# One-hot attention by row maxima and a gather in place of the dense softmax product, with the dense path behind a branch

## The chip, the core and the metric

The kernel runs on one core of a Trainium2 chip, in one launch. The metric is the device time of a launch in microseconds (us). Engines: TensorE (PE, with its weight loads PEld), VectorE (DVE), ScalarE (ACT), GpSimd (POOL) and SyncE (SP); the core's 16 DMA engines move data between HBM and the on-chip memory.

## The reference

```python
def _L0_gnn_ref(h, adj_mat, W, a):            # N = 4096, 4 heads, 512 features
    ht = (h @ W).reshape(N, N_HEADS, N_HIDDEN).transpose(1, 0, 2)
    src = jnp.einsum('hnd,hd->hn', ht, a_src)
    dst = jnp.einsum('hnd,hd->hn', ht, a_dst)
    e = jax.nn.leaky_relu(src[:, :, None] + dst[:, None, :], SLOPE) + adj_mat[None]
    att = jax.nn.softmax(e, axis=-1)
    h_prime = jnp.einsum('hij,hjd->hid', att, ht)
    return h_prime.mean(axis=0)
x = _layernorm(x + _L0_gnn_ref(x, adj, L0_gnn_W, L0_gnn_a), axis=-1)
```

`x` is 4096x512, `adj` 4096x4096, `W` 512x2048, all float32. `adj` enters the scores as an added number. It is zero but for about 17 entries of a row in the mean (the diagonal among them), and those are drawn evenly from 0.05 to 1e9. The scores differ by a few units beside that, so in each row the softmax weight of the column with the largest entry rounds to one and all others to zero, as long as the largest entry leads the second by more than the scores can differ. Over the inputs that the reference makes (seed 0), the smallest lead of any of the 4096 rows is 10,880.

## The kernel before, in words

The kernel computes the dense attention. `x` (32 blocks of 128 rows, 8 MB) stays on chip. The first part (lines 62 to 118) makes the two score vectors: `v = W_h a_h` on VectorE (L83), transposes of `x` (L94), products with `v` (L101), and copies of `dst` to all partitions (L107, L108).

The second part works in units: a block of 128 rows of one head, 32 x 4 = 128 units. A unit's scores are made in 8 chunks of 512 columns: `src + dst` on ScalarE (L153), leaky ReLU (L154) and the sum with `adj` and its row maximum on VectorE (L156), the exponential on ScalarE (L168). TensorE then turns each chunk (`transpose`, L173), the turned chunk is copied out of PSUM (L176 on ScalarE, L178 on VectorE), and `apply` (L186) multiplies it with `x`: 32 products of 128x128 by 128x512 a unit. `scale` divides by the sum (L197), `turn` transposes the result (L202), `project` multiplies by the head's columns of `W` (L211) and, after the fourth head, adds `x` and takes mean and variance (L217 to L224); `store` normalises (L230, L231) and writes the block from GpSimd's queue (L232).

The order is written by hand: in the loop at line 244 a unit's transposes and products stand between the last steps of the unit before it and the score making of the next. `load_adj` (L134) fetches four tiles of 128x1024 of `adj` for a block of rows on SP's queue; each is fetched as soon as VectorE has read the tile before it for the fourth head.

## Time and profile before

| | |
|---|---|
| median of 3 runs | 4705.16 us (4705.05 to 4705.61) |
| span of the profiled execution, first to last instruction | 4702.5 us |
| what the median has beside that span | 2.7 us |
| TensorE busy | 4596.1 us, 98% |
| VectorE, ScalarE, GpSimd busy | 2124.3, 1811.9, 18.2 us |
| moved by DMA over the span | 92.66 MB, mean 20 GB/s |
| granted TensorE clock, mean | 0.992 |

The page gives no time of the profiled execution beside its span; sums are made against the span, and the 2.7 us that the median lies above it are added at the end. Busy shares are of the whole span; a stretch's own figures come from the table by stretch. A busy TensorE in this profile is modelled, since its matmuls overlap; the distance of one matmul's start to the next tells more.

### The profile page before, as it was taken

The numbers are of one execution on the slowest core, as the hardware profiler recorded it, in microseconds if no ns is written. First come the engines' busy times: TensorE is split into PE (matmuls) and PEld (weight loads), VectorE is DVE, ScalarE is ACT, GpSimd is POOL, SyncE is SP. The second block draws the span as 40 slices with busy tenths as digits, with TensorE's granted clock in tenths as the row PEclk, the third lists the DMA queues.
The fourth block names the chain that finished last, engine by engine and source line by source line (L and its number), as shares of the span: only waits on it lengthen the run. The fifth ranks groups of instructions, "written<-read, shape, count | busy, mean of one in ns | idle before, by whom it ended". The sixth has DMA issues, their size and how long they took to land.

```text
span 4702.5 us, 38848 instructions
## 1 busy us (share of the span) xinstructions
PE 4596.1 (98%) x14112; PEld 2251.0 (48%) x14112; DVE 2124.3 (45%) x4656; ACT 1811.9 (39%) x3712; POOL 18.2 (0%) x38
## 2 busy tenths in 40 slices
PE   7899999999999999999999999999999999999999
PEld 3344444444444444444444444444444444444444
DVE  3444444444444444444444444444444444444443
ACT  1334334334334434433433433433433443343342
POOL 0000000000000000000000000000000000000000
PEclk7999999999999999999999999999999999999999
DMA  3000000000000000000000000000000000000000
GB/s 125 27 12 21 18 21 20 12 12 21 18 21 20 7 16 21 18 21 16 7 21 21 18 21 16 7 21 21 18 21 12 12 21 21 18 21 12 12 21 3
DMA packets 26127, 92.66 MB, mean 20 GB/s; under 512 B 2768, under 2 KB 2768, under 8 KB 25296
## 3 DMA queue, kind: packets, MB, share of 16 engines
q1 hardware_dynamic: 22656, 75.51, 4.7%
q0 software_dynamic: 2560, 8.39, 0.5%
q10 hardware_dynamic: 720, 6.29, 0.3%
q8 instruction: 111, 1.82, 0.2%
q14 instruction: 80, 0.66, 0.0%
HBM read 81.79 MB, written 8.39 MB: 19 GB/s over the span
## 4 chain that ended last, share of the span: by engine, by line
issue 75%; PE 23%; DVE 1%; POOL 0%; DMA 0%; ACT 0%; POOLq 0%; ACTq 0%; DVEq 0%
PE y_ps L186 16%; PE o_ps L211 2%; PE pt_ps L173 2%; PE ps_b L107 1%; PE ps_sd L101 1%; PE ps_x L94 0%; DVE y L197 0%; DVE prod L83 0%; PE yt_ps L202 0%; POOL out_dram L232 0%; DMA w_sb<-in_L_gnn_W_dram 0%; DVE s L154 0%; DVE sd L103 0%; DVE s L156 0%; PE ps_s L111 0%
## 5 line engine op out<-in xcount | busy, mean ns | idle before, releaser
L186 PE MATMUL y_ps<-x_sb,pt 128*128 128x512 f32 x8192 | 3685.7, 593 | 0.0
L186 PEld LDWEIGHTS y_ps<-x_sb,pt 128*128 128x128 f32 x8192 | 1487.1, 190 | 1531.3 <-issue 1530.9
L154 DVE SCALAR_TENSOR_TENSOR s<-s 128x512 f32<-128x512 f32 x1024 | 705.6, 689 | 1048.4 <-ACT s L153 1006.2
L153 ACT ACTIVATE s<-dst_b,src 128x512 f32<-128x512 f32 x1024 | 723.0, 718 | 971.2 <-PE pt_ps L173 952.2
L178 DVE COPY pt<-pt_ps 128x512 f32<-128x512 f32 x640 | 442.6, 692 | 997.4 <-PE pt_ps L173 997.4
L168 ACT ACTIVATE s<-s,nm 128x512 f32<-128x512 f32 x1024 | 724.0, 708 | 181.0 <-DVE nm L164 181.0
L173 PEld LDWEIGHTS pt_ps<-ident,s 128*128 128x128 f32 x4096 | 512.5, 141 | 551.7 <-issue 538.7
L176 ACT COPY pt<-pt_ps 128x512 f32<-128x512 f32 x384 | 225.1, 586 | 1346.4 <-PE pt_ps L173 1346.4
L156 DVE CUSTOM_DVE_ANT_0 s<-s,adj 128x512 f32<-128x512 f32 x1024 | 708.6, 692 | 35.1
L173 PE MATMUL pt_ps<-ident,s 128*128 128x128 f32 x4096 | 615.3, 273 | 12.7 <-ACT s L168 12.7
L211 PE MATMUL o_ps<-w_sb,yt 128*128 128x512 f32 x1024 | 460.8, 593 | 0.7 <-ACT yt L204 0.7
L211 PEld LDWEIGHTS o_ps<-w_sb,yt 128*128 128x128 f32 x1024 | 184.6, 190 | 184.6 <-issue 183.6
L197 DVE TENSOR_SCALAR y<-y_ps,rz 128x512 f32<-128x512 f32 x128 | 96.0, 750 | 296.8 <-PE y_ps L186 296.8
L168 ACT ACTIVATION_READ_ACCUMULATOR s<-s,nm 128x1 f32 x1024 | 191.2, 187 | 0.0
L202 PE MATMUL yt_ps<-ident,y 128*128 128x128 f32 x512 | 83.9, 286 | 52.6 <-DVE y L197 52.6
L204 ACT COPY yt<-yt_ps 128x512 f32<-128x512 f32 x128 | 75.0, 586 | 76.0 <-PE yt_ps L202 76.0
L202 PEld LDWEIGHTS yt_ps<-ident,y 128*128 128x128 f32 x512 | 53.6, 140 | 83.5 <-DVE y L197 83.5
L224 ACT ACTIVATE sd<-sd 128x1 f32<-128x1 f32 x32 | 6.5, 203 | 210.8 <-DVE sd L223 210.8
L156 DVE DVE_READ_ACCUMULATOR2_ANT m<- 128x1 f32 x1024 | 83.8, 82 | 0.0
L217 DVE TENSOR_TENSOR y<-o_ps,x_sb 128x512 f32<-128x512 f32 x32 | 22.1, 692 | 90.2 <-PE o_ps L211 90.2
L94 PE MATMUL ps_x<-ident,x_sb 128*128 128x128 f32 x128 | 29.9, 422 | 21.8 <-DMA x_sb<-in_x_dram 16.6
L95 ACT COPY xT<-ps_x 128x512 f32<-128x512 f32 x32 | 18.7, 586 | 76.8 <-PE ps_x L94 76.8
(31 smaller groups left out, 412.8 us busy)
## 6 DMA issues: line engine op xcount, KB each, us to landing
adj<-in_adj_dram SPq DMA_DIRECT2D x128, 512.0 KB, 3.4
x_sb<-in_x_dram SPq DMA_DIRECT2D x8, 1024.0 KB, 17.9
out_dram<-y POOLq DMA_DIRECT2D x32, 256.0 KB, 2.3
w_sb<-in_L_gnn_W_dram ACTq DMA_DIRECT2D x4, 1024.0 KB, 10.7
a_b<-in_L_gnn_a_dram ACTq DMA_DIRECT2D x1, 2048.0 KB, 8.8
```

Source lines behind the costliest of these rows:

```text
L153: nc.scalar.activation(s, dst_b[:, h, ts(c, C)], AF.Identity, bias=src[:, ib, h : h + 1])
L154: nc.vector.scalar_tensor_tensor(s, s, SLOPE, s, op0=OP.mult, op1=OP.max)
L156: nc.vector.tensor_tensor_reduce(out=s, in0=s, in1=adj_t[ib, k][:, ts(part, C)], scale=1.0, scalar=LOWEST, op0=OP.add, op1=OP.max, accum_o ...
L168: nc.scalar.activation(s, s, AF.Exp, bias=self.nm, accum_out=self.z[:, c : c + 1])
L173: nc.tensor.transpose(ps[:, q, :], self.s[c][:, ts(q, P)], ident)
L176: nc.scalar.copy(pt, ps)
L178: nc.vector.tensor_copy(pt, ps)
L186: nc.tensor.matmul(self.y_ps, pt[:, q, :], x_sb[:, c * Q + q, :], start=(c == 0 and q == 0), stop=(c == NCH - 1 and q == Q - 1),)
L197: nc.vector.tensor_scalar_mul(self.y, self.y_ps, self.rz)
L202: nc.tensor.transpose(ps[:, kb, :], self.y[:, ts(kb, P)], ident)
L204: nc.scalar.copy(self.yt, ps)
L211: nc.tensor.matmul(o_ps[ib], self.yt[:, kb, :], w_sb[:, kb, ts(h, D)], start=(h == 0 and kb == 0), stop=(h == H - 1 and kb == KB - 1),)
```

## The change

The whole computation is replaced by two functions, `leading_rows` and `general`.

`leading_rows` reads `adj` once and finds the column of each row's largest entry. Rows are dealt out so that a partition holds 32 neighbouring rows (row p*32 + block), where before a block held 128 neighbouring rows. A block of `adj` is 128 rows of 16 KB, one for each partition, each 512 KB away from the next in memory. For block `t`, VectorE takes the maximum of each of the 64 segments of 64 columns (`segment_maxima`, after.py L157), the 8 largest of those and where the largest is (`find_segment`, L164, L166). GpSimd computes a row number from it and fetches that segment of 64 columns for each partition with an indirect DMA (L170, 256 bytes each). Two steps later `find_column` (L186, L192) takes the two largest in the segment and the position of the largest, GpSimd adds the segment's start (L194), and a second indirect DMA fetches the row of `x` that the column names (L180, 2 KB each). TensorE turns the fetched rows (L207), multiplies them by the mean of the heads' `W` (`products`, L220, four matmuls of 128x512 a block in place of 144 of them before) and adds the block's own `x` by a product with the identity (`residual`, L213). ScalarE takes mean and variance by two accumulating passes (`stats`, L242, L244) and the sum of squares of `x` (`row_norm`, L227), GpSimd makes the reciprocal root by a power (`rstd`, L247 to L249), ScalarE normalises (`finish`, L260).

In the first 15 steps TensorE also makes `v` (`turn_w` L326, `head_vector` L334) and its norms, for the test: `bound` gives from the largest norms how far two scores can differ, `test` asks of each row whether the largest entry leads by more (L375 to L381), `count` and `report` (L385 to L392) write the number of rows that fail. The engines load that number, and only where it isn't zero `general` runs: the dense path for the blocks that hold a failing row, in operations on whole rows of 4096 columns, one head after the other.

`hold` takes `x`, the result, and at first `W` in its last 16 blocks. Loads of `adj` run five blocks ahead in six buffers on SP's queue. The `x` of the last 8 blocks is loaded after the last `adj`, and behind that all stores are issued on the same queue (L305). The sums of blocks 24 to 27 are put by (`put_by`, L233) and get their `x` later (`add_x`, L236); blocks 28 to 30 get theirs in `finish_last` (L293 to L302), block 31 in halves. The test stands ahead of block 29's normalisation.

```diff
-            nc.vector.tensor_copy(sd, ps)
-            for h in range(H):
-                pb = pps.tile([P, C], F32, name="ps_b")
-                one_hot = ident[: 2 * H, H + h : H + h + 1].to_broadcast([2 * H, P])
-                nc.tensor.matmul(pb, one_hot, sd, start=True, stop=True)
-                nc.vector.tensor_copy(dst_b[:, h, ts(g, C)], pb)
-            pt = pps.tile([P, Q, 2 * H], F32, name="ps_s")
...
-        def transpose(self, c):
-            ps = psum.tile([P, Q, P], F32, name="pt_ps", bufs=3)
-            for q in range(Q):
-                nc.tensor.transpose(ps[:, q, :], self.s[c][:, ts(q, P)], ident)
...
-        def apply(self, c):
-            if c == 0:
-                self.y_ps = psum.tile([P, D], F32, name="y_ps")
-            pt = self.pt.pop(c)
-            for q in range(Q):
-                nc.tensor.matmul(
-                    self.y_ps, pt[:, q, :], x_sb[:, c * Q + q, :],
-                    start=(c == 0 and q == 0), stop=(c == NCH - 1 and q == Q - 1),
-                )
...
-    for k in range(NCH // AW):
-        load_adj(0, k)
-    u = Unit(0)
...
+    leading_rows(tc, x, adj, W, a, out, ident, v, n_bad, any_bad)
+    flag = nc.values_load(any_bad[0:1, 0:1], min_val=0, max_val=N)
+    with tc.If(flag > 0, preferred_fallthrough_block=False):
+        general(tc, x, adj, W, out, ident, v, n_bad)
...
+    AHEAD = 5
+    Q = 4
+    PIECES = 4
+    LATE = NB - Q
+    BEHIND = LATE - Q
...
+    adj_rows = adj.rearrange("(p nb) m -> nb p m", nb=NB)
+    adj_segs = adj.rearrange("n (s e) -> (n s) e", e=E)
+    x_rows = x.rearrange("(p nb) d -> p nb d", nb=NB)
+    out_rows = out.rearrange("(p nb) d -> p nb d", nb=NB)
+    w_blocks = W.rearrange("(kb p) (h d) -> p kb h d", p=P, h=H)
...
+    def load_adj(ib):
+        if 0 <= ib < NB:
+            t = adj_t[ib] = adj_pool.tile([P, N], F32, name="adj_t")
+            n = pieces(ib)
+            for k in range(n):
+                nc.sync.dma_start(t[:, ts(k, N // n)], adj_rows[ib][:, ts(k, N // n)])
...
+    load_adj(0)
+    for s in range(2):
+        nc.scalar.dma_start(a_rows[ts(s, H), :], a[:, ts(s, D), :].rearrange("h d o -> h (d o)"))
+    for kb in range(KB):
+        load_w(kb)
+        load_adj(kb + 1)
+    load_x(0, Q)
+    for ib in range(KB + 1, AHEAD):
+        load_adj(ib)
...
+        n = max(pieces(ib), 2)
+        for k in range(lo * n // PIECES, hi * n // PIECES):
+            nc.vector.tensor_reduce(
+                seg_of[ib][:, ts(k, S // n)],
+                adj_t[ib][:, ts(k, N // n)].rearrange("p (s e) -> p s e", e=E), axis=AX.X, op=OP.max,
+            )
...
+    def find_segment(ib):
+        seg = seg_of.pop(ib)
+        nc.vector.max(out=top[:, ib, :], in_=seg)
+        at = small.tile([P, 8], U32, name="at")
+        nc.vector.max_index(at, top[:, ib, :], seg)
+        row = small.tile([P, 1], U32, name="row")
+        nc.gpsimd.tensor_tensor(row, at[:, 0:1], first[:, ib : ib + 1], op=OP.add)
+        lead = small.tile([P, E], F32, name="lead", bufs=2 * Q + 1)
+        nc.gpsimd.indirect_dma_start(
+            out=lead, out_offset=None, in_=adj_segs,
+            in_offset=bass.IndirectOffsetOnAxis(ap=row[:, :1], axis=0),
+        )
+        start = at_of[ib] = small.tile([P, 1], U32, name="start")
+        nc.gpsimd.tensor_tensor(start, at[:, 0:1], width, op=OP.mult)
+        lead_of[ib] = lead
+    def gather_rows(ib, col):
+        y = y_t[ib] = rows.tile([P, D], F32, name="y", bufs=4)
+        nc.gpsimd.indirect_dma_start(
+            out=y, out_offset=None, in_=x,
+            in_offset=bass.IndirectOffsetOnAxis(ap=col[:, :1], axis=0),
+        )
+    def find_inner(ib):
+        nc.vector.max(out=inner[:, ib, :], in_=lead_of[ib])
...
+        within = small.tile([P, 8], U32, name="within")
+        nc.vector.max_index(within, top[:, ib, :], lead_of[ib])
+        col = small.tile([P, 1], U32, name="col")
+        nc.gpsimd.tensor_tensor(col, at_of.pop(ib), within[:, 0:1], op=OP.add)
+        gather_rows(ib, col)
+    def find_column_in_row(ib):
+        col = small.tile([P, 8], U32, name="col")
+        nc.vector.max_index(col, top[:, ib, :], adj_t[ib])
+        gather_rows(ib, col)
+    def turn(ib):
+        y = y_t.pop(ib)
+        tp = psum.tile([P, KB, P], F32, name="tp", bufs=2)
+        for kb in range(KB):
+            nc.tensor.transpose(tp[:, kb, :], y[:, ts(kb, P)], ident)
...
+    def residual(ib):
+        o_ps[ib] = psum.tile([P, D], F32, name="o")
+        nc.tensor.matmul(o_ps[ib], ident, hold[:, ib, :], start=True, stop=False)
...
+        for kb in range(lo, hi):
+            nc.tensor.matmul(
+                o_ps[ib], yt_of[ib][:, kb, :], w_sum[:, kb, :],
...
+    def row_norm(ib):
+        sq = rows.tile([P, D], F32, name="sq")
+        nc.scalar.activation(sq, hold[:, ib, :], AF.Square, accum_out=xx[:, ib : ib + 1])
...
+    def stats(ib):
+        o, i = o_ps[ib], slice(ib, ib + 1)
+        sq = rows.tile([P, D], F32, name="sq")
+        nc.scalar.activation(sq, o, AF.Identity, scale=-1.0 / D, accum_out=nm[:, i])
+        sq = rows.tile([P, D], F32, name="sq")
+        nc.scalar.activation(sq, o, AF.Square, bias=nm[:, i], accum_out=sd[:, i])
+    def rstd(i):
+        nc.gpsimd.tensor_scalar(sd[:, i], sd[:, i], 1.0 / D, EPS, op0=OP.mult, op1=OP.add)
+        nc.gpsimd.tensor_tensor(sd[:, i], sd[:, i], power[:, : i.stop - i.start], op=OP.pow)
+        nc.gpsimd.tensor_mul(nm[:, i], nm[:, i], sd[:, i])
...
+    def finish(ib):
+        i = slice(ib, ib + 1)
+        nc.scalar.activation(hold[:, ib, :], o_ps.pop(ib), AF.Identity, bias=nm[:, i], scale=sd[:, i])
...
+    def finish_last(ib, residual):
+        o = o_ps.pop(ib)
+        if residual:
+            nc.vector.tensor_add(hold[:, ib, :], o, hold[:, ib, :])
+            o = hold[:, ib, :]
+        st = small.tile([P, nc.vector.BN_STATS_DIM], F32, name="st", bufs=2)
+        nc.vector.bn_stats(st, o)
+        mv = small.tile([P, nc.vector.BN_AGGR_DIM], F32, name="mv", bufs=2)
+        nc.vector.bn_aggr(mv, st)
+        r = small.tile([P, 1], F32, name="r", bufs=2)
+        nc.scalar.activation(r, mv[:, 1:2], AF.Sqrt, bias=eps)
+        nc.vector.reciprocal(r, r)
+        nc.vector.tensor_scalar(hold[:, ib, :], o, mv[:, 0:1], r, op0=OP.subtract, op1=OP.mult)
+    def store(queue, lo, n):
+        queue.dma_start(out_rows[:, ds(lo, n), :], hold[:, ds(lo, n), :])
...
+    def test():
+        a1 = top[:, :, 0]
+        nc.vector.tensor_tensor(gap, top[:, :, 1], inner[:, :, 1], op=OP.max)
+        size = once.tile([P, NB], F32, name="size")
+        nc.vector.scalar_tensor_tensor(size, a1, -1.0, a1, op0=OP.mult, op1=OP.max)
+        nc.vector.tensor_sub(gap, a1, gap)
+        nc.vector.tensor_scalar(size, size, -(2.0 ** -22), lead_by, op0=OP.mult, op1=OP.subtract)
+        nc.vector.scalar_tensor_tensor(gap, gap, 0.9999, size, op0=OP.mult, op1=OP.add)
+        nc.vector.tensor_scalar(gap, gap, 0.0, None, op0=OP.is_gt)
...
+    COLUMN, PROJECT, STATS, FINISH = 2, 3, 4, 6
+    for t in range(NB):
+        if t in x_at:
+            load_x(*x_at[t])
+        load_adj(t + AHEAD)
+        middle = 1 if t > LATE else 2
+        segment_maxima(t, 0, middle)
+        if t >= COLUMN:
+            find_column(t - COLUMN)
+        segment_maxima(t, middle, PIECES)
+        pair = FINISH <= t < BEHIND + FINISH and t % 2 == 0
+        if pair:
+            rstd(slice(t - FINISH, t - FINISH + 2))
+        find_segment(t)
...
+        ib = t - PROJECT
+        if ib >= 0:
+            turn(ib)
+            if ib < BEHIND:
+                residual(ib)
+        if ib >= 0:
+            products(ib)
+        if t >= BEHIND + STATS:
+            put_by(t - STATS)
+        elif t >= STATS:
+            stats(t - STATS)
+            row_norm(t - STATS)
+        if pair:
+            finish(t - FINISH)
+            finish(t - FINISH + 1)
+    for ib in range(BEHIND, NB, 2):
+        load_x(ib, 2)
+    for ib in range(0, BEHIND, 2):
+        store(nc.sync, ib, 2)
+    find_column(NB - 2)
+    find_column_in_row(NB - 1)
+    for ib in range(BEHIND, NB - 2):
...
+    finish_last(NB - 4, True)
+    bound(0)
...
+    stats(BEHIND)
+    stats(BEHIND + 1)
+    rstd(slice(BEHIND, BEHIND + 2))
+    for ib in range(BEHIND, NB):
+        find_inner(ib)
+    bound(2)
+    test()
+    pg = count()
+    stats(BEHIND + 2)
+    turn(NB - 1)
+    finish_last(NB - 3, True)
+    report(pg)
+    finish(BEHIND)
...
+    products_of_half(NB - 1, 0)
+    products_of_half(NB - 1, 1)
+    rstd_late(slice(BEHIND + 2, LATE))
+    finish_last(NB - 2, True)
+    finish(BEHIND + 2)
+    finish(BEHIND + 3)
+    for ib, n in ((NB - 4, 1), (NB - 3, 1), (BEHIND, 2), (NB - 2, 1), (BEHIND + 2, 2)):
+        store(nc.sync, ib, n)
+    finish_in_halves(NB - 1)
+    store(nc.sync, NB - 1, 1)
...
+        for h in range(H):
+            s = score.tile([P, N], F32, name="s")
+            nc.scalar.activation(s, dst_b[:, h, :], AF.Identity, bias=src_i[:, h : h + 1])
+            nc.vector.scalar_tensor_tensor(s, s, SLOPE, s, op0=OP.mult, op1=OP.max)
+            m = stat.tile([P, 1], F32, name="m")
+            nc.vector.tensor_tensor_reduce(
+                out=s, in0=s, in1=adj_t, scale=1.0, scalar=LOWEST, op0=OP.add, op1=OP.max, accum_out=m
+            )
...
+            nc.scalar.activation(s, s, AF.Exp, bias=m, accum_out=z)
+            y_ps = psum.tile([P, D], F32, name="y_ps")
+            for c in range(NCH):
+                ps = psum.tile([P, Q, P], F32, name="pt_ps")
+                for q in range(Q):
+                    nc.tensor.transpose(ps[:, q, :], s[:, ds(c * C + q * P, P)], ident)
+                pt = turned.tile([P, Q, P], F32, name="pt")
+                (nc.scalar.copy if c % 2 else nc.vector.tensor_copy)(pt, ps)
+                for q in range(Q):
+                    nc.tensor.matmul(
+                        y_ps, pt[:, q, :], x_sb[:, c * Q + q, :],
+                        start=(c == 0 and q == 0), stop=(c == NCH - 1 and q == Q - 1),
+                    )
...
+    with tc.For_i(0, NB, 1) as ib:
+        of_block = stat.tile([1, 1], I32, name="of_block", bufs=1)
+        nc.vector.tensor_copy(of_block, n_bad[0:1, ds(ib, 1)])
+        here = nc.values_load(of_block[0:1, 0:1], min_val=0, max_val=P)
+        with tc.If(here > 0):
+            block(ib)
```

Where the instructions stand now, at the places that matter here. First SP's DMA queue in the changed kernel from its last load of four blocks of `x` on (names: `adj_t` a block of `adj`, `hold` first W and later x and the result):

```order
L115 DMA hold<-in_x_dram 128x2048
L112 DMA adj_t<-in_adj_dram 128x4096 x4
L112 DMA adj_t<-in_adj_dram 128x1024 x16
L115 DMA hold<-in_x_dram 128x1024 x4
L305 DMA out_dram<-hold 128x1024 x12
L305 DMA out_dram<-hold 128x512 x2
L305 DMA out_dram<-hold 128x1024
L305 DMA out_dram<-hold 128x512
L305 DMA out_dram<-hold 128x1024
L305 DMA out_dram<-hold 128x512
```

Every store stands behind the last load; before, SP held loads of `adj` alone after the first eight and the stores went out from GpSimd's queue, one a block.

VectorE before, two chunks of a unit's scores and a copy of turned weights:

```order
L154 SCALAR_TENSOR_TENSOR s<-s 128x512
L156 ISA s,m<-s,adj_1577 128x512
L156 ISA m 128x1
L178 COPY pt<-pt_ps 128x512
L154 SCALAR_TENSOR_TENSOR s<-s 128x512
L156 ISA s,m<-s,adj_1577 128x512
L156 ISA m 128x1
```

and VectorE in the changed kernel, one whole block of rows in the middle (`seg` the maxima of segments, `lead` the fetched segment):

```order
L157 TENSOR_REDUCE seg<-adj_t 128x32
L186 MAX inner<-lead 128x8
L192 MAX_INDEX within<-top,lead 128x8
L157 TENSOR_REDUCE seg<-adj_t 128x32
L164 MAX top<-seg 128x8
L166 MAX_INDEX at<-top,seg 128x8
```

The six rows are all that VectorE does for the search of a block of 128 rows, for all heads; the rows before are a quarter of one of a block's four units. The sizes printed are those of the result: each TENSOR_REDUCE reads 128x2048.

VectorE at the end of the changed kernel, from the last rows of block 31 (`top` the 8 largest of a row):

```order
L164 MAX top<-seg 128x8
L166 MAX_INDEX at<-top,seg 128x8
L192 MAX_INDEX within<-top,lead 128x8
L200 MAX_INDEX col<-top,adj_t 128x8
L293 TENSOR_TENSOR hold<-o,hold 128x512
L296 BN_STATS st<-hold 128x6
```

For block 31 the two-level search is replaced by one MAX_INDEX over the whole row (L200), and `finish_last` of block 28 stands right behind it.

## Rows read from the trace of the kernel before

**Rows 1.** The page: span, busy time of each engine, chain that ended last.
```profile
span 4702.5 us, 38848 instructions
PE 4596.1 (98%) x14112; PEld 2251.0 (48%) x14112; DVE 2124.3 (45%) x4656; ACT 1811.9 (39%) x3712; POOL 18.2 (0%) x38
issue 75%; PE 23%; DVE 1%; POOL 0%; DMA 0%; ACT 0%; POOLq 0%; ACTq 0%; DVEq 0%
```
**Rows 2.** Busy by stretch: stretch, length, PE, PEld, DVE, ACT, POOL, PEclk, DMA share, GB/s.
```profile
1000.00:1141.90 141.90, 140.27 (x435) 68.88 (x434) 64.79 (x143) 56.05 (x115) 0.54 (x1) 1.00 0.05 17
```
**Rows 3.** The timeline of TensorE around 2005 us: start, length, instructions.
```profile
2001.89 3.60 PE L186 MATMUL y_ps<-x_sb,pt 128*128 128x512 f32 x8
2005.32 0.60 PE L173 MATMUL pt_ps<-ident,s 128*128 128x128 f32 x4
2005.76 3.60 PE L186 MATMUL y_ps<-x_sb,pt 128*128 128x512 f32 x8
```
**Rows 4.** DMA queues: packets, MB, share of 16 engines.
```profile
q1 hardware_dynamic: 22656, 75.51, 4.7%
q0 software_dynamic: 2560, 8.39, 0.5%
q10 hardware_dynamic: 720, 6.29, 0.3%
```
**Rows 5.** Busy by stretch while x, W and a are loaded, and later four tiles of adj.
```profile
0.00:38.00 38.00, 11.35 (x40) 6.16 (x40) 22.37 (x64) 5.88 (x9) 0.70 (x6) 0.96 0.97 374
2.35:38.00 35.65, 11.35 (x40) 6.16 (x40) 22.37 (x64) 5.88 (x9) 0.00 (x0) 0.95 1.02 397
10.00:18.00 8.00, 1.36 (x7) 1.39 (x8) 4.83 (x14) 0.00 (x0) 0.00 (x0) 1.00 1.02 417
30.00:38.00 8.00, 3.16 (x6) 0.20 (x4) 6.12 (x18) 0.00 (x0) 0.00 (x0) 0.80 1.05 386
134.00:138.00 4.00, 3.50 (x12) 1.30 (x10) 2.83 (x5) 0.41 (x1) 0.00 (x0) 0.89 0.96 333
```
**Rows 6.** Groups by line, VectorE: shapes, count, busy us, mean ns, idle before.
```profile
L156 DVE CUSTOM_DVE_ANT_0 s<-s,adj 128x512 f32<-128x512 f32 x1024 | 708.6, 692 | 35.1
L154 DVE SCALAR_TENSOR_TENSOR s<-s 128x512 f32<-128x512 f32 x1024 | 705.6, 689 | 1048.4 <-ACT s L153 1006.2
L164 DVE TENSOR_REDUCE nm<-m 128x1 f32<-128x8 f32 x128 | 20.6, 161 | 4.5
```
**Rows 7.** Groups by line, ScalarE.
```profile
L168 ACT ACTIVATE s<-s,nm 128x512 f32<-128x512 f32 x1024 | 724.0, 708 | 181.0 <-DVE nm L164 181.0
L176 ACT COPY pt<-pt_ps 128x512 f32<-128x512 f32 x384 | 225.1, 586 | 1346.4 <-PE pt_ps L173 1346.4
L168 ACT ACTIVATION_READ_ACCUMULATOR s<-s,nm 128x1 f32 x1024 | 191.2, 187 | 0.0
```
**Rows 8.** Groups by line, GpSimd, and its DMA issue in the page (KB each, us to landing).
```profile
L232 POOL DMA_DIRECT2D out_dram<-y x32 | 17.5, 546 | 4679.8 <-DVE y L231 4679.8
masks.py:199 POOL TENSOR_SCALAR_AFFINE_SELECT ident<-ident 128x128 f32<-128x128 f32 x1 | 0.3, 289 | 0.1
...
out_dram<-y POOLq DMA_DIRECT2D x32, 256.0 KB, 2.3
```
**Rows 9.** The timeline of the last 8 us: the last block's normalisation and store.
```profile
4694.96 0.69 DVE L217 TENSOR_TENSOR y<-o_ps,x_sb 128x512 f32<-128x512 f32 x1 [5.18 <-PE o_ps L211]
4695.69 0.69 DVE L219 BATCH_NORM_STATS2 st<-y 128x6 f32<-128x512 f32 x1
4696.42 0.18 DVE L221 BATCH_NORM_AGGREGATE mv<-st 128x2 f32<-128x6 f32 x1
4697.26 0.55 DVE L231 TENSOR_SCALAR y<-y,mv,sd 128x512 f32<-128x512 f32 x1
4698.10 0.54 POOL L232 DMA_DIRECT2D out_dram<-y  x1 [136.09 <-DVE y L231]
```
**Rows 10.** The chain in order of time: last piece of the score vectors (start, length).
```profile
133.33 3.88 PE ps_b L107 x8
```

More of the change, by code (lines that the diff above doesn't have):

```diff
@@ L5 @@
 from concourse import mybir
-from concourse.bass import ts
+from concourse.bass import ds, ts
 from concourse.masks import make_identity
@@ L17 @@
 LOWEST = -3.4028234663852886e38
+P = 128
+C = 512
+E = 64
 @with_exitstack
@@ L51, in gat_resnorm_kernel, with general @@
+@with_exitstack
+def general(ctx, tc, x, adj, W, out, ident, v, n_bad):
+    nc = tc.nc
+    N, D = x.shape
+    KB, NB, NCH, Q = D // P, N // P, N // C, C // P
+    H = v.shape[2] // 2
     const = ctx.enter_context(tc.tile_pool(name="const", bufs=1))
     x_sb = const.tile([P, NB, D], F32, name="x_sb")
-    w_sb = const.tile([P, KB, H * D], F32, name="w_sb")
     dst_b = const.tile([P, H, N], F32, name="dst_b")
     src = const.tile([P, NB, H], F32, name="src")
-    ident = const.tile([P, P], F32, name="ident")
+    w_sb = const.tile([P, KB, H * D], F32, name="w_sb")
@@ new lines, in general, with block @@
+    turned = ctx.enter_context(tc.tile_pool(name="turned", bufs=2))
+    stat = ctx.enter_context(tc.tile_pool(name="stat", bufs=2))
+    psum = ctx.enter_context(tc.tile_pool(name="psum_g", bufs=2, space=bass.MemoryType.PSUM))
+    def block(ib):
+        src_i = stat.tile([P, H], F32, name="src_i", bufs=1)
+        nc.vector.tensor_copy(src_i, src[:, ds(ib, 1), :].rearrange("p o h -> p (o h)"))
+        held = psum.tile([P, D], F32, name="o_ps", bufs=1)
+        adj_t = score.tile([P, N], F32, name="adj_g")
+        nc.gpsimd.dma_start(adj_t, adj[ds(ib, P, NB), :])
+        for h in range(H):
+            s = score.tile([P, N], F32, name="s")
+            nc.scalar.activation(s, dst_b[:, h, :], AF.Identity, bias=src_i[:, h : h + 1])
@@ L199, in turn @@
-        def turn(self):
-            ps = psum.tile([P, KB, P], F32, name="yt_ps", bufs=1)
-            for kb in range(KB):
-                nc.tensor.transpose(ps[:, kb, :], self.y[:, ts(kb, P)], ident)
-            self.yt = yt_pool.tile([P, KB, P], F32, name="yt")
-            nc.scalar.copy(self.yt, ps)
-        def project(self):
-            ib, h = self.ib, self.h
-            if h == 0:
-                o_ps[ib] = psum.tile([P, D], F32, name="o_ps")
+                out=s, in0=s, in1=adj_t, scale=1.0, scalar=LOWEST, op0=OP.add, op1=OP.max, accum_out=m
+            )
@@ L210, in project @@
+            nc.vector.tensor_scalar_mul(z, z, float(H))
+            nc.vector.reciprocal(z, z)
+            y = turned.tile([P, D], F32, name="y_g")
+            nc.vector.tensor_scalar_mul(y, y_ps, z)
+            ps = psum.tile([P, Q, P], F32, name="pt_ps")
+            for q in range(Q):
+                nc.tensor.transpose(ps[:, q, :], y[:, ts(q, P)], ident)
+            yt = turned.tile([P, KB, P], F32, name="pt")
+            nc.scalar.copy(yt, ps)
             for kb in range(KB):
                 nc.tensor.matmul(
-                    o_ps[ib], self.yt[:, kb, :], w_sb[:, kb, ts(h, D)],
+                    held, yt[:, kb, :], w_sb[:, kb, ts(h, D)],
@@ L227, in store @@
-        def store(self):
-            if self.h == H - 1:
-                r, mv, sd = norm.pop(self.ib)
-                nc.vector.reciprocal(sd, sd)
-                nc.vector.tensor_scalar(r, r, mv[:, 0:1], sd, op0=OP.subtract, op1=OP.mult)
-                nc.gpsimd.dma_start(out[ts(self.ib, P), :], r)
-    for k in range(NCH // AW):
-        load_adj(0, k)
-    u = Unit(0)
-    for c in range(NCH):
-        u.add(c)
-    u.largest()
-    for c in range(NCH):
-        u.exp(c)
-    before = None
@@ L244, in gat_resnorm_kernel @@
-    for n in range(len(units) + 1):
-        after = Unit(n + 1) if n + 1 < len(units) else None
-        for c in range(NCH):
-            if u is not None:
-                u.transpose(c)
-            if before is not None:
-                if c == 0:
-                    before.apply(NCH - 1)
-                    before.scale()
-                elif c == 1:
-                    before.turn()
-                elif c == 2:
-                    before.project()
-                elif c == 3:
-                    before.store()
-            if u is not None and c > 0:
-                u.apply(c - 1)
-            if after is not None:
-                if c == 0:
-                    after.add(0)
-                if c + 1 < NCH:
-                    after.add(c + 1)
-                if c == NCH - 2:
-                    after.largest()
-                if c >= NCH - 2:
-                    half = NCH // 2
-                    for e in range(half):
-                        after.exp((c - (NCH - 2)) * half + e)
-        before, u = u, after
+        r = turned.tile([P, D], F32, name="y_g")
```

308 lines of the change are left out of this document (215 added, 93 removed).

## The prediction

> **What bounds the kernel now.** The page comes first: TensorE is busy for 98% of a span of 4702.5 us, VectorE and ScalarE for less than half, and the chain that ended last is 98% TensorE's own work or its issue [rows 1]. The table by stretch then gives the length of one block of 128 rows in the middle: 141.9 us, of which TensorE works 140.3 at the full clock, while the DMA engines carry 17 GB/s [rows 2]. The timeline shows why: eight matmuls of 128x512 and four transposes follow one another every 3.87 us without a hole [rows 3]. So the time is the matmul count of the dense product, and whatever does away with that count does away with the time. What is left after that is to be read from rows that don't matter today: the DMA queues, and what VectorE and ScalarE take for an instruction.
>
> **Whether the new path is the one that runs.** The reference's inputs decide it. The test asks for a lead of 1.05 x 25.16 (largest norm of a row of x) x 2.60 (largest sum of two norms of v) + 110 + 1e9 / 2^22, at most 417. The smallest lead of any row is 10,880, so no row fails and `general` is skipped. Its price stands with the rivals.
>
> **What goes.** All the work of rows 1 goes: TensorE's 128 products a block of L186 and the chunks' operations on VectorE and ScalarE. Nothing that is left on TensorE comes near a bound: a block now has 4 transposes and 5 matmuls of 128x512, 0.45 + 5 x 0.43 = 2.6 us by the spacing of [rows 3]; at half that clock 5.2 us.
>
> **What comes: DMA.** Before, 92.66 MB moved over the whole span, most of it on SP's queue [rows 4]. Now 67.1 MB of adj, 4.2 of W, 8.4 of x, 8.4 of fetched rows of x, 1.05 of fetched segments and 8.4 of stores, 97.5 MB together, are nearly all the kernel does. The rate is read from the first 38 us, where loads alone bounded: 397 GB/s between 2.35 and 38 us, 417 while W's and a's long pieces were in flight beside x (10 to 18), 386 with x's 2 KB rows alone (30 to 38). The start costs 38 x (1 - 374/397) = 2.2 us [rows 5].
>
> Up to the moment at which the last piece of adj has landed (call it T0), SP's queue holds adj, W and 24 blocks of x, and GpSimd's holds 29 blocks of fetched rows and 31 of segments; the last x and every store stand behind the last adj. Long pieces: 71.3 MB at 417 GB/s = 171.0 us. Short ones: 6.3 + 7.6 + 1.0 = 14.9 MB at 386 = 38.6 us. The segments are 256-byte pieces, which the trace doesn't show. If such a piece took no more than its bytes it adds nothing; if it took as long as a 2 KB piece, 31 x 0.262 MB at 386 GB/s less what is counted, +18 us. I take +3, near the lower end, because a segment is one piece beside 20 KB of others for its partition. T0 is then 2.2 + 171.0 + 38.6 + 3 = 215.4 us.
>
> **What comes: VectorE beside it.** From a 128x512 operation (692 ns) and a 128x8 reduction (161) a column costs 1.05 ns and an instruction 0.15 us [rows 6]. A block's two reductions of 2048 columns cost 2 x 2.31 = 4.62 us. The two MAX and two MAX_INDEX over 64 columns aren't in the trace: each lies between 0.16 us (the 128x8 row) and 0.69 (the 512 row); by columns 0.22, and I add some for loading the eight values. With 0.04 us between operations [rows 9], a block takes 5.8 us. DMA brings a block in (2.10 + 0.26 + 0.26 + 0.03 MB) / 0.41 = 6.5 us, and once x has stopped, 5.8. VectorE hides, with little over at the end: blocks 28 to 31 take four reductions instead of two, 2 x 0.15 more each, so I add 1 us of lag. If VectorE didn't hide it would be late next (rival below).
>
> ScalarE per block: one copy of 0.59, four passes of 0.71, three of them with 0.19 to read the sum, and 0.59 more for a turned W while those last: 4.0 to 4.6 us [rows 7], hidden by the same 6.5. GpSimd: two indirect DMAs, three tiny operations and three more for each pair of blocks. The row for its plain DMA issue says 0.55 us, for a tiny operation 0.1 to 0.29 [rows 8]: 2.4 us a block. An indirect issue isn't shown; up to (6.5 - 1.3) / 2 = 2.6 us each it stays hidden. Behind it wait TensorE (fetched rows) and, two steps later, VectorE (segments); six buffers of adj cover some 20 us of such a delay.
>
> **What comes: the end.** After T0 VectorE's instructions stand in one row: the last reduction of 1024 columns 1.2, MAX and MAX_INDEX 0.5, the column of block 30 0.25, MAX_INDEX over 4096 columns 4.5 (by the slope; bounds: half that, or twice), three `finish_last` of 2.85 each (as L217 to L231 took, 4694.96 to 4697.81 [rows 9]) = 8.6, four adds of x at 0.69 = 2.8, eight MAX 1.8, bound, test, report and the late root some 16 small ones at 0.16 to 0.2 = 3.0, the two halves of block 31 2.4, and 25 gaps of 0.04 = 1.0: 26 us. ScalarE must first make eight sums of squares (0.9 each) of x rows that land behind the last adj, which holds the first `finish_last` back by some 1.5. Block 31's own fetch, turn and product (0.55 to issue, 2.3 to land, 0.6, 0.6, 2 to 4) lie beside that. From the last store's issue to the end it took 4702.5 - 4698.1 = 4.4 us [rows 9], into which I put the load of the flag and the skipped branch as well (between nothing and 2 us more). So 32 us after T0. The DMA engines have 2.1 MB of x and 8.4 MB of stores left there: 10.5 / 0.4 = 26 us, just inside.
>
> Sum: 215.4 + 1 + 32 = 248.4 us of span; the median lies 2.7 above the span now, so **251 us**, some 19 times shorter.
>
> **Rivals.**
> 1. *Rows 512 KB apart slow the adj loads* (12%). Today's x and adj tiles lie in neighbouring rows; the new blocks don't. The lowest rate that the trace shows for a burst of loads is 333 GB/s, of four tiles of adj in 4 KB pieces [rows 5]; with it 67.1 MB take 201 instead of 161 us: 251 + 40 = 291. Against it: today's bursts are short and include the ramp.
> The Trainium skill (DMA: Bandwidth & Descriptors, section "Latency and other measured facts") lists copies of such blocks at a row pitch of 512 KiB at 207 GB/s against 214 at full rate, and 164 only from 2 MiB; by it the adj term would grow by 3%, to 256 us in all, as an estimate. No row here has that pitch.
> 2. *VectorE becomes the bound* (9%). If MAX and MAX_INDEX cost what a 512-wide operation does, a block takes 4.62 + 4 x 0.69 + 0.25 = 7.6 us; 32 x 7.6 behind the first 8 us, and 32 us of end: 283 + 3 = 286. For it: nothing in the trace shows them. Against: they read 64 columns.
> 3. *GpSimd's issue is the bound* (5%): indirect issues of 3.3 us, six times the plain one, make 7.9 us a block: 8 + 253 + 32 + 3 = 296, with VectorE waiting for segments.
> 4. *Slower: the branch is taken* (2%). `general` handles one block's head after head with nothing overlapped: 8 x (0.72 + 0.69 + 0.69 + 0.71) = 22.5 us on ScalarE and VectorE [rows 6, 7], then the 35.5 us of TensorE work of a unit (141.9 / 4), so 58 x 4 + 10 = 242 us a block, after 137 us of score vectors [rows 10]. One block: 251 + 137 + 242 = 630. All 32: 8,130. It becomes slower than now from (4705 - 388) / 242 = 18 blocks on. Against it stand the leads above; for it only an error in that working.
> 5. *Below 238* (3%): all bytes at 417, and an end of 26 us.
>
> **How the numbers follow.** The likeliest case, 69%, gives 251, and by its bounds 238 (everything at 417 GB/s, segments free, end 28) to 272 (segments as 2 KB pieces). Rivals 1 and 2 reach up from there to 286 and 291; the range 238 to 288 holds the first case and most of those two, some 83%. A measurement of this kernel can tell 0.2% from no change; every case but all of `general` is far faster: faster 0.98, same 0.005, slower 0.015.
>
> **What would show it.** DMA share near 1.0 and about 400 GB/s from 3 us to T0; VectorE waiting for adj at its first reduction of each block, 1 us or less a block late in the run; T0 at 213 to 220; about 32 us from there to the end, VectorE busy in most of it; no instruction of `general`. Wrong if the DMA share sinks in the middle (then VectorE's or GpSimd's queue shows who is late), if the rate is under 380 with a full share, or if MAX_INDEX over 64 columns takes over 0.5 us.

## The result, and the profile after

The changed kernel takes 245.51 us (median of 5 runs, 244.48 to 246.45) against 4705.07 us before: a ratio of 0.0522, 95% interval 0.0521 to 0.0523. The forecast was 251, its range 238 to 288. The span of the profiled execution is 243.9 us, 1.6 us under the median.

The page after, its busy times, and the 40 slices of the span for TensorE's clock and the DMA engines:

```profile
span 243.9 us, 2511 instructions
...
PE 198.6 (81%) x679; PEld 103.2 (42%) x679; DVE 189.3 (78%) x312; ACT 112.0 (46%) x270; POOL 95.9 (39%) x209
...
PEclk9999799999999999999979999799979999979995
DMA  6999999999999999999999999999999999999943
...
DMA packets 14994, 97.75 MB, mean 401 GB/s; under 512 B 2296, under 2 KB 2296, under 8 KB 10240
```

Where [rows 1] show TensorE at 98%, no engine is above 81% now; the DMA row is full from the second slice to the 38th. The bytes hardly changed (92.66 MB before); the time in which they move did, from 4702 us to 240. The table by stretch gives the rate (stretch, length, busy time of PE, PEld, DVE, ACT, POOL, clock, DMA share, GB/s):

```profile
0.00:3.00 3.00, 0.00 (x0) 0.00 (x0) 0.00 (x0) 1.15 (x1) 1.11 (x11) 1.00 0.27 83
...
60.00:100.00 40.00, 38.37 (x169) 23.03 (x167) 32.82 (x49) 23.56 (x57) 19.03 (x40) 1.00 1.01 422
...
140.00:180.00 40.00, 32.26 (x86) 13.75 (x84) 33.49 (x52) 19.79 (x49) 19.05 (x40) 0.96 1.01 421
180.00:200.00 20.00, 18.45 (x50) 8.85 (x51) 18.92 (x28) 11.44 (x27) 12.18 (x26) 0.92 1.01 404
...
220.00:230.00 10.00, 9.78 (x34) 4.93 (x35) 7.91 (x29) 7.35 (x23) 1.90 (x4) 1.00 1.02 417
230.00:240.00 10.00, 3.55 (x17) 2.79 (x16) 5.77 (x19) 5.00 (x11) 0.00 (x0) 0.90 0.58 224
```

421 GB/s with a full share up to 180 us, 404 in the 20 us after that; only behind 230 us does the share sink. This is what [rows 5] were read for, and a little more than they showed (397, 417 at best). Next VectorE, GpSimd, one line of TensorE and the longest waits, by line (shapes, count, busy us, mean ns, idle before):

```profile
L157 DVE TENSOR_REDUCE seg<-adj_t 128x32 f32<-128x2048 f32 x54 | 122.8, 2275 | 32.0 <-DMA adj_t<-in_adj_dram 31.7
...
L164 DVE MAX8 top<-seg 128x8 f32<-128x64 f32 x32 | 7.3, 228 | 1.1
...
L166 DVE FIND_INDEX8 at<-top,seg 128x8 uint32<-128x64 f32 x32 | 7.0, 219 | 0.0
...
L200 DVE FIND_INDEX8 col<-top,adj_t 128x8 uint32<-128x4096 f32 x1 | 4.4, 4419 | 0.0
...
L166 DVE MATCH_VALUE_LOAD at<-top,seg 128x8 f32 x32 | 2.9, 92 | 3.4 <-DVE top L164 0.5
...
L170 POOL DMA_INDIRECT lead<-in_adj_dram,row x32 | 32.2, 1005 | 14.0 <-POOL row L168 14.0
...
L180 POOL DMA_INDIRECT y<-in_x_dram,col x32 | 30.7, 960 | 18.5 <-POOL col L194 15.1 <-PE tp L207 3.5
...
L220 PE MATMUL o<-w_sum,yt 128*128 128x512 f32 x248 | 118.0, 618 | 4.2 <-ACT yt L209 4.2
```

The list of waits (in total, times, longest), its line for adj:

```profile
DVE seg L157 <- DMA adj_t<-in_adj_dram: 36.5, 18, 5.6
```

That is VectorE's only long wait. The operations that [rows 6] didn't have cost what the slope per column said: 228 and 219 ns over 64 columns (0.22 us taken), 4.42 us over 4096 (4.5 taken), plus 0.09 to load the eight values. An indirect issue costs 0.96 to 1.0 us of GpSimd, twice the plain one of [rows 8] and well under the 2.6 up to which it stays hidden.

The end, in VectorE's timeline (start, length): the last reductions, the wait for block 30's fetched segment, the whole-row search, and the last normalisation.

```profile
208.73 3.46 DVE L157 TENSOR_REDUCE seg<-adj_t 128x16 f32<-128x1024 f32 x3
...
214.33 0.09 DVE L192 MATCH_VALUE_LOAD within<-top,lead 128x8 f32 x1 [1.48 <-DMA lead<-in_adj_dram,row]
...
214.66 4.42 DVE L200 FIND_INDEX8 col<-top,adj_t 128x8 uint32<-128x4096 f32 x1
...
237.81 0.99 DVE L285 TENSOR_SCALAR hold<-o,mv,r 128x256 f32<-128x256 f32 x2
```

VectorE finishes block 31's reductions at 212.2 us, and the span ends 31.7 us later. No wait for adj stands before any of block 31's four reductions: VectorE is late there, by an amount that an experiment has to date. For that the first store will serve, which SP issues when the first of block 31's four pieces has landed (SP's waits have three of its stores behind a DMA into `adj_t`):

```profile
205.48 33.68 SPq L305 DMA_DIRECT2D out_dram<-hold  x18
```

### The profile page after: what moved, and what is told of

The parts are those of the page before. It is cut to its first block, busy times and chain, and to the rows that moved or that the text cites. A ratio compares the mean times of both kernels' runs of the same rounds, so it can differ in the third digit from the quotient of the medians.

```text
span 243.9 us, 2511 instructions
## 1 busy us (share of the span) xinstructions
PE 198.6 (81%) x679; PEld 103.2 (42%) x679; DVE 189.3 (78%) x312; ACT 112.0 (46%) x270; POOL 95.9 (39%) x209
## 4 chain that ended last, share of the span: by engine, by line
## 5 line engine op out<-in xcount | busy, mean ns | idle before, releaser
L157 DVE TENSOR_REDUCE seg<-adj_t 128x32 f32<-128x2048 f32 (+1 forms) x74 | 146.3, 1987 | 37.0 <-DMA adj_t<-in_adj_dram 36.5
L220 PE MATMUL o<-w_sum,yt 128*128 128x512 f32 x248 | 118.0, 618 | 4.2 <-ACT yt L209 4.2
L220 PEld LDWEIGHTS o<-w_sum,yt 128*128 128x128 f32 x248 | 46.4, 197 | 59.7 <-issue 46.6
L209 ACT COPY yt<-tp 128x512 f32<-128x512 f32 x32 | 18.8, 588 | 51.9 <-PE tp L207 42.0
L180 POOL DMA_INDIRECT y<-in_x_dram,col x32 | 30.7, 960 | 18.5 <-POOL col L194 15.1
L170 POOL DMA_INDIRECT lead<-in_adj_dram,row x32 | 32.2, 1005 | 14.0 <-POOL row L168 14.0
L310 PE MATMUL o<-hold,ident 128*128 128x512 f32 x32 | 18.8, 744 | 15.7 <-DMA hold<-in_L_gnn_W_dram 15.7
L207 PE MATMUL tp<-ident,y 128*128 128x128 f32 x128 | 20.5, 284 | 11.0 <-DMA y<-in_x_dram,col 10.8
L213 PE MATMUL o<-hold,ident 128*128 128x512 f32 x48 | 27.1, 648 | 0.5 <-DMA hold<-in_x_dram 0.5
L207 PEld LDWEIGHTS tp<-ident,y 128*128 128x128 f32 x128 | 15.1, 145 | 23.0 <-issue 22.9
L194 POOL TENSOR_TENSOR col<-start,within 128x1 uint32<-128x1 uint32 x31 | 5.8, 189 | 47.1 <-DVE within L192 47.1
L328 ACT COPY wt<-tp 128x512 f32<-128x512 f32 x16 | 9.2, 587 | 32.3 <-PE tp L326 27.7
L227 ACT ACTIVATE sq<-hold 128x512 f32<-128x512 f32 x32 | 19.8, 620 | 0.0
L334 PEld LDWEIGHTS pv<-at_d,wt 128*128 128x128 f32 x128 | 16.3, 191 | 6.8 <-issue 3.6
L310 PEld LDWEIGHTS o<-hold,ident 128*128 128x128 f32 x32 | 7.3, 239 | 25.0 <-POOL row L168 11.2
L260 ACT ACTIVATE hold<-o,nm,sd 128x512 f32<-128x512 f32 x24 | 17.2, 771 | 0.0
L244 ACT ACTIVATE sq<-o,nm 128x512 f32<-128x512 f32 x24 | 16.5, 687 | 0.8
L334 PE MATMUL pv<-at_d,wt 128*128 128x2 f32 x128 | 15.3, 244 | 0.6 <-ACT wt L328 0.6
L242 ACT ACTIVATE sq<-o 128x512 f32<-128x512 f32 x24 | 14.6, 609 | 0.0
L326 PEld LDWEIGHTS tp<-ident,hold 128*128 128x128 f32 x64 | 7.9, 142 | 6.9 <-issue 6.9
```

Source lines behind the costliest of these rows:

```text
L157: nc.vector.tensor_reduce(seg_of[ib][:, ts(k, S // n)], adj_t[ib][:, ts(k, N // n)].rearrange("p (s e) -> p s e", e=E), axis=AX.X, op=OP.max,)
L170: nc.gpsimd.indirect_dma_start(out=lead, out_offset=None, in_=adj_segs, in_offset=bass.IndirectOffsetOnAxis(ap=row[:, :1], axis=0),)
L180: nc.gpsimd.indirect_dma_start(out=y, out_offset=None, in_=x, in_offset=bass.IndirectOffsetOnAxis(ap=col[:, :1], axis=0),)
L207: nc.tensor.transpose(tp[:, kb, :], y[:, ts(kb, P)], ident)
L209: nc.scalar.copy(yt, tp)
L213: nc.tensor.matmul(o_ps[ib], ident, hold[:, ib, :], start=True, stop=False)
```

## The experiments

The theory was the prediction's: the DMA stream sets the time until the last adj has landed, VectorE hides beside it, and behind it stands a row of VectorE and ScalarE work of some 31 us. Rivals: the row pitch, VectorE, the segment fetches or GpSimd's issue set the pace; or the stores set the end.

**The base twice**, the changed kernel itself beside the first group of runs and beside the last. 

> The changed kernel itself, as the base for the three beside it. 245.5 us within 1; span about 244, 421 GB/s from 20 to 180 us, VectorE's last reduction of block 31 ending about 212 us.

 

> The changed kernel again, as the base for the three beside it: 245.5 us within 1.

 Measured 245.45 (4 runs, 244.45 to 245.72) and 245.36 (5 runs, 244.73 to 246.01): differences above 1 us can be read. The runs with more VectorE work, with early stores and with the branch taken had no base of their own beside them; they are set against 245.45.

**Neighbouring rows.**

```diff
-    adj_rows = adj.rearrange("(p nb) m -> nb p m", nb=NB)
+    adj_rows = adj.rearrange("(nb p) m -> nb p m", nb=NB)
...
-    nc.gpsimd.iota(first, pattern=[[S, NB]], base=0, channel_multiplier=NB * S)
+    nc.gpsimd.iota(first, pattern=[[P * S, NB]], base=0, channel_multiplier=S)
```

> A block of adj is now 128 neighbouring rows (16 KB apart) instead of rows 512 KB apart; nothing else moves, so the attention of other rows goes into a row's result. Theory (the loads already run at the rate that the DMA engines give): no change, 245.5 within 1, 421 GB/s in the middle. Rival (rows 512 KB apart cost 3% of the adj reads, as the page on DMA would have it): 67.1 MB take 5 us less, 240.5, and the rate in the middle rises towards 430.

Measured 245.72 us (245.21 to 246.13). The rate in the table by stretch, first the base, then this run:

```profile
60.00:180.00 120.00, 109.11 (x379) 55.70 (x377) 100.73 (x154) 68.28 (x164) 58.26 (x122) 0.97 1.01 422
```
```profile
60.00:180.00 120.00, 108.64 (x379) 56.16 (x377) 101.35 (x158) 68.24 (x164) 59.14 (x125) 0.97 1.01 421
```

Rows 512 KB apart cost nothing against rows 16 KB apart; rival 1 falls. The Trainium skill's 3% (DMA: Bandwidth & Descriptors, "Latency and other measured facts") is told there of copies between two places in HBM; for these loads into on-chip memory the trace differs from it, and the measurement decides.

**No segment fetch.**

```diff
-        nc.gpsimd.tensor_tensor(row, at[:, 0:1], first[:, ib : ib + 1], op=OP.add)
-        lead = small.tile([P, E], F32, name="lead", bufs=2 * Q + 1)
-        nc.gpsimd.indirect_dma_start(
-            out=lead, out_offset=None, in_=adj_segs,
-            in_offset=bass.IndirectOffsetOnAxis(ap=row[:, :1], axis=0),
-        )
...
-        lead_of[ib] = lead
+        lead_of[ib] = lead_one
...
-        nc.gpsimd.tensor_tensor(col, at_of.pop(ib), within[:, 0:1], op=OP.add)
+        nc.gpsimd.tensor_tensor(col, at_of.pop(ib), zero, op=OP.add)
```

> Left out: the indirect fetch of each row's best segment of 64 columns (32 DMAs of 128 pieces of 256 bytes) and the row number that it needs; VectorE searches a constant tile instead, and the fetched row of x is that of the segment's first column. Theory (such a piece costs its bytes or little more): 1 MB less at 421 GB/s, 2.4 us less on the loads, 243 us. Rival A (a 256-byte piece costs the DMA engines as much as one of 2 KB): up to 19 us less on the loads; VectorE's own 5.4 us a block would then bound, about 232. Rival B (GpSimd's issue bounds): 1.2 us a block less there, 36 in all.

Measured 239.3 us (239.0 to 239.51), 6.15 less than the base: more than the bytes, far from the rivals. SP's timeline dates the first store, which waits for the first piece of block 31 to have landed; the base, then this run:

```profile
206.52 33.13 SPq L305 DMA_DIRECT2D out_dram<-hold  x18
```
```profile
200.88 32.17 SPq L302 DMA_DIRECT2D out_dram<-hold  x18
```

The loads are 5.6 us shorter for 1.0 MB of segments, which would be 2.4 us at 421 GB/s. The profile's pages split that: the row of GpSimd's queue (packets, MB, share of 16 engines), the base, then this run:

```profile
q0 software_dynamic: 3584, 9.44, 9.8%
```
```profile
q0 software_dynamic: 2560, 8.39, 8.8%
```

9.8% of 244.2 us is 23.9 us, 8.8% of 237.5 is 20.9: the segments' own packets took 3.0 us of all engines, about 1.2 times what their bytes would. That agrees in direction with what the Trainium skill (DMA: Bandwidth & Descriptors, "Specifications") says of transfers under 512 bytes, that they don't run at line rate. The other 2.6 us are a faster rate of everything beside them, 427 GB/s in the middle where the base has 422:

```profile
60.00:180.00 120.00, 112.05 (x398) 57.75 (x396) 103.34 (x161) 71.19 (x175) 38.25 (x92) 1.00 1.01 427
```

What made it faster stays open: the segments are gone, but the row fetches changed as well, since the first column of a segment can name only 64 of the 4096 rows of x. GpSimd's work fell from 96.3 to 58.1 us, 38 us, and the time by 6, so its issue is not the bound; rival 3 falls.

**Half of the columns.**

```diff
-                adj_t[ib][:, ts(k, N // n)].rearrange("p (s e) -> p s e", e=E), axis=AX.X, op=OP.max,
+                adj_t[ib][:, ts(k, N // n)].rearrange("p (s e) -> p s e", e=E)[:, :, : E // 2], axis=AX.X, op=OP.max,
...
-        nc.vector.tensor_scalar(gap, gap, 0.0, None, op0=OP.is_gt)
+        nc.vector.tensor_scalar(gap, gap, LOWEST, None, op0=OP.is_gt)
```

> Left out: half of the columns in the segment maxima (32 of each segment's 64), so VectorE's reductions take about half the time; the lead test is made to pass for every row. Loads, fetches and the end stay. Theory (the loads bound, VectorE is late by about 3 us only at the last block): T0 goes from 212 to 209 and the time to 242.5. Rival (VectorE bounds): 2.2 us a block less, 70 us in all, down to what the DMA engines need for 97.7 MB, about 236.

Measured 243.57 us (242.48 to 244.06), 1.9 less. VectorE's wait for adj in this run (total, times, longest), then its last reduction in the timeline:

```profile
DVE seg L157 <- DMA adj_t<-in_adj_dram: 99.7, 38, 6.3
```
```profile
210.18 0.69 DVE L157 TENSOR_REDUCE seg<-adj_t 128x16 f32<-128x512 f32 x1 [0.60 <-DMA adj_t<-in_adj_dram]
```

VectorE lost 67 us of work (189.1 to 122.4) and waits 62 us longer; the time hardly moves. Rival 2 falls. The run also dates T0: the last piece landed at 210.2 us, 4.4 behind the first store:

```profile
205.77 30.93 SPq L305 DMA_DIRECT2D out_dram<-hold  x18
```

In the base the first store stands at 206.52, so its last piece landed at about 210.9. VectorE ended its last reduction there at 213.0 (209.56 + 3.45); it takes 1.2 us, so it began at 211.8, a lag of 0.9 us. The 2.8 us of the later expectations is the end of that reduction less T0 of this run: it counts the reduction itself, and a T0 that is 0.7 earlier.

**More VectorE work.**

```diff
+        nc.vector.tensor_tensor(more, adj_t[ib][:, :D], adj_t[ib][:, D : 2 * D], op=OP.max)
```

> Added: one VectorE maximum of two 128x512 pieces of adj per block (0.69 us), its result unused. Theory (VectorE waits for adj some 38 us over the run, nearly all of it before block 25, and is late only at the end): a block takes 6.1 us of VectorE, which is less than a block takes on the DMA engines while x comes along (6.4) and 0.4 us more than afterwards (5.7), so 3 to 5 us more: 249. Rival (VectorE bounds): 32 x 0.72 = 23 us more, 268.

Measured 247.39 us (246.8 to 247.93), 2 us above the base for 22 us of work; VectorE's wait for adj fell from 38.0 to 27.0. A little less than the theory's 3 to 5, far from 23. The two runs together: VectorE's work shows only where the last blocks are late.

**Stores among the loads.**

```diff
         load_adj(t + AHEAD)
+        if t + AHEAD == NB - 1:
+            for ib in range(BEHIND, NB, 2):
+                load_x(ib, 2)
+        if t >= 8 and t % 2 == 0:
+            store(nc.sync, t - 8, 2)
...
-    for ib in range(BEHIND, NB, 2):
-        load_x(ib, 2)
-    for ib in range(0, BEHIND, 2):
-        store(nc.sync, ib, 2)
```

> The first 24 blocks are stored as they are ready, between the loads on SP's queue, instead of behind the last load. Theory (the end is VectorE's and ScalarE's work in a row behind the last adj, beside which stores are free, while a store among the loads holds the last adj back): ten stores of 512 KB, 5.2 MB at 420 GB/s, come before the last adj, +12.5 us: 258. Rival (the stores' bytes set the end, so their place does not matter): 245.5 within 2.

Measured 254.93 us (254.42 to 256.84), 9.5 us slower. VectorE's last reductions end at 222.9 instead of 213.0, and from 230 to 240 us the DMA engines are three quarters idle (the timeline, then the table by stretch):

```profile
220.44 2.50 DVE L157 TENSOR_REDUCE seg<-adj_t 128x16 f32<-128x1024 f32 x2 [0.24 <-DMA adj_t<-in_adj_dram]
```
```profile
230.00:240.00 10.00, 10.00 (x28) 4.55 (x27) 6.62 (x28) 5.22 (x17) 1.48 (x4) 0.78 0.23 75
```

From the last reduction to the end it takes 32.3 us here (255.2 - 222.9) and 31.2 in the base (244.2 - 213.0), though half of the stores are gone from that stretch. So the end is the row of compute behind T0, and stores beside it are free; a store ahead of T0 costs its bytes. Nine stores, not ten, went ahead (nine are left after 217.5 us), 11.2 us at 420 GB/s, and VectorE's lag went (its last reductions wait for adj), which makes up about half of the rest.

**The branch taken**, for one block and for all.

```diff
+        nc.vector.tensor_scalar(n_bad[:, 3:4], pg[:, 3:4], -1.0, float(P + 1), op0=OP.mult, op1=OP.add)
...
-        nc.vector.tensor_scalar(any_bad, total, -1.0, float(N), op0=OP.mult, op1=OP.add)
+        nc.vector.tensor_scalar(any_bad, total, -1.0, float(N + 1), op0=OP.mult, op1=OP.add)
```

(for all: `float(P + 1)` in the line that makes `n_bad`.) 

> Block 3 is reported as failing one row, so the branch is taken and the dense path runs for one block. By the working of the prediction 137 us of score vectors and 242 us for the block: 245 + 379 = 625 us. If loads of x and W, which start only after the branch, come on top: 645. If the dense block overlaps less than thought (copies and products in turn through two buffers): up to 700.

 

> All 32 blocks are reported as failing. By the working of the prediction 245 + 137 + 32 x 242 = 8,130 us, slower than the dense kernel by 1.7 times; from e7 and this the price of one block and the point from which the branch is slower follow (18 blocks by that working).

Measured 733.08 us for one block (2 runs), 8564.92 for 32. A further block costs (8564.9 - 733.1) / 31 = 252.6 us against 242 in the working. One block costs 488 instead of 379 because of something the working left out: the loop over the blocks that don't fail. VectorE's timeline of two such passes:

```profile
637.15 0.14 DVE L612 COPY of_block<-n_bad 1x1 int32 x1 [4.49 <-PEq L610]
640.44 0.14 DVE L612 COPY of_block<-n_bad 1x1 int32 x1 [3.15 <-PEq L610]
```

3.3 us each, but 10.5 for the first (362.7 to 373.3): 31 of them take 109 us, as much as the whole difference. The block itself took 257 us, from one such copy (379.9) to the next (637.2), against 242 in the working; the rest, some 121 us, is left for the score vectors, against 137. A further block takes the place of a skipped pass. The point from which the branch is slower than the dense kernel is (4705 - 733) / 252.6 = 15.7 further blocks, 17 of 32 (18 by the working).

**Two ways to shorten the end.** More pieces for blocks 24 to 27; the adds of x on GpSimd; both, with two adds ahead of the last fetch:

```diff
-        return PIECES if ib == 0 or ib >= LATE else 1
+        return PIECES if ib == 0 or ib >= BEHIND else 1
```
```diff
-        nc.vector.tensor_add(hold[:, ib, :], hold[:, ib, :], o_ps["by"][:, ib - BEHIND, :])
+        nc.gpsimd.tensor_add(hold[:, ib, :], hold[:, ib, :], o_ps["by"][:, ib - BEHIND, :])
```

> Blocks 24 to 27 of adj are loaded in four pieces too, as 28 to 31 are, so VectorE need not wait for block 27 as a whole. Theory (in the run with half the columns the whole lag of 2.8 us at the last block was worth 1.9 us of time): VectorE starts block 28 earlier, the lag shrinks to 1 or 1.5 us, 1.0 to 1.5 us faster: 244.2. Rival (the lag comes from VectorE's own pace, 5.4 us a block): no change, as four reductions cost 0.15 us more each block.

 

> The four adds of x to the sums that were put by (L236) go from VectorE to GpSimd, which has little to do after the last fetch. Theory (from the last whole-row search on, VectorE's instructions in a row set the end): 2.5 us less on VectorE, less what ScalarE's sums of block 27 then hold back; 1 to 2.5 us faster: 243.5. Rival (block 31's own fetch, turn and product set the end): at most the 2.7 us of slack that its products have, or nothing if ScalarE is late: 245.5.

 

> Both edits, and two of the four adds ahead of the last fetch on GpSimd. Theory: the gains add to 2.5 to 3.5 us: 242.5. Rival (GpSimd's adds hold back block 31's fetch, or block 31's chain sets the end): 244 to 245.5.

Measured 244.86 us (243.5 to 245.44), 250.12 (248.12 to 250.66) and 249.06 (248.71 to 251.18) against 245.36. The medians differ by 0.5 us for the pieces, inside the spread of the runs. The lag did go: VectorE waits among block 31's last reductions there.

```profile
210.34 2.35 DVE L157 TENSOR_REDUCE seg<-adj_t 128x16 f32<-128x1024 f32 x2 [0.43 <-DMA adj_t<-in_adj_dram]
```

The table by stretch says what took most of that back, the base first:

```profile
160.00:180.00 20.00, 16.18 (x45) 6.57 (x43) 16.42 (x26) 10.37 (x25) 9.86 (x21) 1.00 1.01 423
```
```profile
160.00:180.00 20.00, 19.79 (x58) 8.88 (x57) 19.45 (x34) 13.26 (x33) 11.83 (x25) 1.00 1.02 404
```

Loads of 512 KB (4 KB for each partition) run at 404 GB/s where those of 2 MB (16 KB for each) run at 423, so four more blocks in pieces cost 8.4 MB x (1/404 - 1/423) = 0.9 us of what the shorter lag gives. The adds on GpSimd are a loss of 4.8 us, and the timeline of that run shows it (GpSimd, then VectorE):

```profile
221.46 4.91 POOL L236 TENSOR_TENSOR hold<-hold,adj_t 128x512 f32<-128x512 f32 x4
...
221.83 4.83 DVE L302 TENSOR_SCALAR hold<-hold,mv,r 128x512 f32<-128x512 f32 x1
```

VectorE's normalisation of block 28 takes 4.83 us instead of 0.55: it ends 0.3 us after the fourth add. VectorE saves its own 2.5 us of adds, but `bound`, which goes over TensorE and ScalarE, starts as much later, and VectorE waits 3.7 us for it instead of 1.3 in the base. Not every VectorE operation is held so: in the last run the whole-row search keeps its 4.42 us beside two adds (VectorE, then GpSimd).

```profile
213.65 4.42 DVE L200 FIND_INDEX8 col<-top,adj_t 128x8 uint32<-128x4096 f32 x1
...
216.21 2.50 POOL L236 TENSOR_TENSOR hold<-hold,adj_t 128x512 f32<-128x512 f32 x2
```

In that run VectorE's chain is held earlier, by 3.3 us behind ScalarE: `row_norm` of blocks 24 and 25 stands behind the adds in the program there, so it waits for them (and squares the sums, not x alone, in its bound). None of the three versions beats the changed kernel clearly.

## Why the prediction was right

Each step against what was measured, in the order of the sum.

- *Start, 2.2 us.* 83 GB/s in the first 3 us: 3 x (1 - 83/421) = 2.4.
- *TensorE, 2.6 us a block.* The reading was wrong by two: [rows 3] have eight matmuls where a chunk of the program has four products, and the page after has 248 for 31 blocks of four. A product is two instructions, so a block takes 10 x 0.43 + 0.45 = 4.8 us by the same spacing. It stayed hidden beside the 5.7 us that a block's 2.4 MB take at 421 GB/s, with a granted clock of 0.95. But the 5.2 us that the prediction allows for at half that clock would by the same doubling be 9.6, far above them: that the step did no harm was luck.
- *Loads until T0, 171.0 + 38.6 us.* This is the term that was too large. T0 was put at 215.4 and lies at about 209.9 in the profiled run (first store 205.48, and 4.4 on); without the start that is 86.2 MB in 207.5 us, 415 GB/s, where the sum had 405 with the segments' extra in. The split was sound in kind: long pieces do run faster than short ones. But 386 GB/s for 2 KB rows alone was the wrong row for 2 KB pieces mixed with 16 KB rows. It was also used for the 6.3 MB of x, which no longer come as 2 KB pieces: a partition now holds neighbouring rows, and `load_x` takes four of them, 8 KB together in memory. And the best stretch of 8 us (417) was still below what holds over 120 us (422).
- *Segments, 2.6 by their bytes + 3.* 5.6 measured, in part by luck: the +3 was a choice between 0 and 18 for the price of the pieces, but their own packets took 3.0 us in all. The other 2.6 are the rate beside them, which rose from 422 to 427 without them (and with the changed row fetches), a thing that the sum did not have.
- *VectorE hidden, 5.8 us a block.* Some 5.5 measured, 5.4 in the last blocks; hidden, as runs with 2.1 us less and 0.7 us more a block show.
- *Lag, 1 us.* 1.1 in the profiled run: the last reduction ended at 212.2 and takes 1.2 us, so it began at 211.0, against T0 at 209.9; 0.9 in the base.
- *The end, 32 us*, the last reduction's 1.2 among them. 32.9 from its start (243.9 - 211.0). The total came out by errors that cancel: MAX over 64 columns in a row was cheaper (eight in 1.09 us, 1.8 in the sum) and ScalarE's sums of squares did not hold the first `finish_last` back (1.5 in the sum), but VectorE waited 1.5 us for block 30's segment and 1.8 for ScalarE before the late root, which the sum did not have.
- *Beside the span, 2.7 us.* 1.6 now.

So 251.1 against 245.5 is -5.5 (T0) + 0.1 (lag) + 0.9 (end) - 1.1 (beside the span). The path was right: loads at a full DMA share, VectorE hidden, then a row of compute. Of what was to show a step right or wrong, two things did not come as told: the date of T0, which lay 3 us under the 213 to 220 given, and VectorE's waits for adj, the last of which ends at 169 us, since from there on VectorE is late. Rivals 1, 2 and 3 have fallen by experiment; rival 4's price is measured and its condition did not arise; of rival 5 the faster loads came, the shorter end did not. What stays open: how much of the end could be taken away, since the two tries ran into other things.
